# Input norm and first taps on GpSimd, output norms on ScalarE, 4 KB read-back, PSUM banks from a table, a new order

## The chip, the cores and the metric

The kernel runs on one core of a Trainium2 chip. A core has five engines that run at the same time, each with its own instruction queue, taken strictly in order: TensorE (PE; weight loads are shown as PEld), VectorE (DVE), ScalarE (ACT), GpSimd (POOL) and SyncE (SP), which here only issues DMA transfers. Engines wait for one another through semaphores. The metric is the device time of one execution in microseconds; the median of several executions counts.

## The reference

The input `x` is [16, 256, 64, 64] in float32: 16 images, 256 channels, 4096 pixels. Two layers, each added to its input:

```python
# --- layer 0: linear attention ---
x = x + _L0_conv_ref(_gn(x), g_norm, w_qkv, w_out, b_out, g_out)
# --- layer 1: two of four experts for each image ---
x = x + _L1_conv_ref(_gn(x), router_w, router_b, dw_w, dw_b, pw_w, pw_b)
```

`_gn` is a group norm over 32 groups of 8 channels. Layer 0 scales every pixel to unit length over its channels, projects it to q, k and v (4 heads of 32), takes a softmax of q over the head's channels and of k over the pixels, forms a 32 x 32 context for each head, multiplies, projects back to 256 channels and scales every pixel to unit length again. Layer 1 takes the mean over the pixels, a small router, the best two of four experts, and adds their weighted sums; an expert is a 3 x 3 depthwise convolution, GELU (the exact one) and a 256 x 256 pointwise product:

```python
def _expert(x, dw_k, dw_b, pw_k, pw_b):
    h = conv_depthwise_3x3(x, dw_k) + dw_b
    h = gelu(h, approximate=False)
    return einsum('bchw,oc->bohw', h, pw_k) + pw_b
```

## The kernel before

`block_kernel` checks whether the logits of the softmax stay small enough for exponentials without a maximum; they do here, and `pipelined_path` is what runs. `general_path` stands in the program but is not executed.

`pipelined_path` writes its order out by hand. Every step is a small function that issues a few instructions (`norm`, `turn_x`, `out_norm`, `tap1`, ...). A list of rows says which steps exist for which image `b`, group of 512 pixels `g` (8 in an image), quarter of the image `j` (4) or half `h` (2). `place` gives each row a due time from the table `PLAN` (about 3100 entries, many for one image and one group alone), the rows are sorted by it (line 1648), and the instructions are issued in this order. An image has `PERIOD` = 64 units; several images are under way at once: while image b goes through the experts, image b+1 is in the attention and image b+2 is being read for its statistics. So every engine's queue mixes work of up to three images, and the sorted order decides what stands behind what.

The steps that matter here, in the order of one image:

- `load_a` and `load_b` (lines 974, 977): the image is read twice from HBM, in pieces of 128 channels x 512 pixels (`xa` for the statistics, `xb` for the norm), and a third time by `load_x1` into `ring`, a ring of 7 quarter images in which the residual is kept and the output is built.
- `stats` (982) and the steps up to `gn0_bias`: scale `sc` and bias `bi` of the first group norm, one of each for every channel.
- `norm` (1019): `xg = xb * sc + bi`, on VectorE for images 0 and 1 (`EARLY`) and on ScalarE for the other 14; two instructions of 128 x 512 for a group.
- `turn_x` (1030) transposes `xg` on TensorE into the bank `px`; `x_squares` (1039) and `token_scale` (1055) make the pixel's scale `r`, the latter on GpSimd, by a multiply and a power (lines 959 and 960); `x_keep` (1046) writes the scaled transposed pixels to `xt`.
- `project` (1060) makes q and k (bank `pq`), `evacuate` (1071) takes the exponential with scale `r` on ScalarE into `e`, `context` (1079) accumulates on TensorE; `q_sum` (1092, VectorE), `q_norm` (1097, GpSimd), `q_turn` (1103, TensorE, bank `ptq`) and `q_keep` (1109, ScalarE) prepare the normalised q.
- `mix_a` to `mix_c`: once for an image, the context times the output weights (`mw`).
- `attend` (1155): TensorE, two tiles of 128 x 256 into the bank `po`. `out_squares` (1164) on ScalarE and `out_scale` (1172) on GpSimd make the scale `s`. `out_norm` (1176): `ob = po * s`, on ScalarE (two instructions of 128 x 256, line 1181) for images 0, 1 and 15, on VectorE (one of 128 x 512, line 1183) for the other 13; 16 tiles of 128 x 512 in an image.
- `out_turn` (1185) transposes `ob` back (bank `tr`), `out_add` (1193) adds it to `ring` on VectorE, `square_sums` (1202) gathers the second group norm's sums on ScalarE.
- Router: `gn1_sums` to `pick_bias`, short instructions, mostly on VectorE. The chosen experts' weights are fetched by `fetch`, `lace` (GpSimd copies them into `taps`) and `fetch_pw`.
- First 128 channels of the depthwise convolution, on TensorE: `pad0` writes the normalised, padded image; `lay` (1379) stores it in HBM; `spread` (1384) reads it back as overlapping patches into `xr`, in two transfers for each half of the partitions (48 and 6 rows); `conv0` (1422) multiplies by the banded `taps` into the banks `dw`; `gelu0` (1441); `put` (1446) stores the result in the HBM buffer `hids`; `take` (1454) reads it back with the channels on the partitions into `hp`, in four transfers for a half image, each of 32 partitions with one row of 4096 numbers (16 KB) for a partition.
- Second 128 channels, on VectorE: `pad1` (1402); `start1` (1464) writes the first tap with the bias, `acc = pd1 * ds0 + bias`, 128 x 1024, on ScalarE; `tap1` (1472) adds the other eight taps, 128 x 1024 each, two tensors in SBUF as inputs; `gelu1` (1479) on ScalarE.
- `pointwise` (1484): for each quarter and each 128 output channels, the products of both experts and both halves of the channels into two banks `pw`; `residual` (1512) adds bias and residual on VectorE into `ring`; `store` (1520).

All PSUM tiles but the context's come from one pool of 7 banks, `bank` (971), which hands them out in turn: a new tile takes the bank of the tile seven requests earlier and waits until that tile's last reader is done.

Of the kernel before, what the change touches and what calls it, by code (L numbers as in the profile page):

```python
# [10 lines left out]
FP = mybir.dt.float32  # L11
AF = mybir.ActivationFunctionType
ALU = mybir.AluOpType
# [3 lines left out]
P = 128  # L17
# [32 lines left out]
NU = P // (2 * CB)  # L50
NXR = 4
# [9 lines left out]
    "load_x1": 2.02, "mean": 1.19, "means": 13.36, "dev": 13.73, "devs": 17.34, "scale": 17.85,  # L61
    "bias": 21.91, "in_lead": 26.39, "norm0": -8.96, "norm1": -3.87, "turn_x0": 0.72, "x_sq0": 1.77,
    "x_sq1": 2.31, "turn_x1": 1.43, "x_sq2": 3.45, "x_sq3": 3.25, "token": 4.42, "x_keep0": 5.53,
    "x_keep1": 5.77, "x_keep2": 5.97, "x_keep3": 6.03, "project0": 3.18, "evacuate0": 6.05,
    "project1": 3.64, "evacuate1": 6.46, "project2": 3.67, "evacuate2": 6.47, "project3": 4.06,
    "evacuate3": 6.58, "context": 9.48, "q_sum": 8.22, "q_norm": 11.06, "q_turn": 14.73,
    "q_keep": 16.31, "mix_a": 9.53, "mix_turn": 10.09, "mix_v": 11.08, "mix_vv": 11.63,
    "mix_b": 11.82, "mix_out": 13.35, "mix_c": 13.91, "mix_lead": 16.02, "attend0": -1.14,
    "out_sq0": -0.04, "out_sq1": 0.35, "out_scale0": 0.42, "out_norm0": 1.58, "attend1": -0.28,
    "out_sq2": 1.31, "out_sq3": 1.37, "out_scale1": 3.18, "out_norm1": 4.28, "out_turn0": 5.64,  # L70
    "out_add0": 6.51, "sq_sums0": 8.92, "out_turn1": 6.16, "out_add1": 7.06, "sq_sums1": 9.17,
    "sums1": 9.6, "means1": 9.77, "scale1": 10.52, "router": 10.97, "route": 11.89, "choose": 13.68,
    "pick_taps": 21.03, "route_lead": 21.97, "weigh": 29.78, "pick_bias": 41.15, "pad1": -10.35,
    "start0": -0.53, "tap01": 1.33, "tap02": 1.57, "tap03": 1.59, "tap04": 1.87, "tap05": 2.54,
    "tap06": 4.55, "tap07": 4.74, "tap08": 6.14, "gelu10": 13.51, "start1": 1.94, "tap11": 3.52,
    "tap12": 8.13, "tap13": 8.14, "tap14": 8.54, "tap15": 9.95, "tap16": 12.84, "tap17": 13.06,
    "tap18": 14.42, "gelu11": 15.46, "pw00": 16.32, "pw01": 16.45, "pw02": 17.78, "pw03": 17.83,
    "pw10": 16.09, "pw11": 16.24, "pw12": 19.85, "pw13": 20.43, "residual00": 19.8,
    "residual01": 20.37, "store0": 32.19, "residual10": 22.5, "residual11": 23.44, "store1": 26.19,
    "in_first": 0.96, "in_more": 1.71, "q_first": 3.46, "out_first": 27.07, "out_more": 37.75,  # L80
    "q_less": 0.19, "load_a0": -17.62, "load_a1": -6.91, "load_b0": -15.96, "load_b1": -6.67,
    "stats0": -13.55, "stats1": -1.94, "load_weights": 58, "scale_weights": -7.03,
    "end_pw00": 135.48, "end_pw01": -49.35, "end_pw02": 69.96, "end_pw03": 337.87,
    "end_residual00": 3.29, "end_residual01": 66.1, "end_pw10": 115.56, "end_pw11": -47.98,
    "end_pw12": -196, "end_pw13": -114.87, "end_residual10": -13.43, "end_residual11": 88.85,
    "x_0": 0.99, "x_1": -0.21, "x_2": -0.19, "x_e1": 5.09, "x_e2": 4, "route_0": -3.83,
    "route_1": 0.32, "route_2": -0.55, "route_e1": -1.2, "route_e2": -0.21, "out_0": -5.81,
    "out_1": -0.4, "out_2": 0.09, "out_e1": -1.85, "out_e2": -0.87, "q_0": -7.21, "q_1": -2.22,
    "q_2": 0.4, "q_e1": -1.65, "q_e2": -0.57, "in_0": -22.93, "in_1": 7.98, "in_2": 2.65,
    "in_e1": -1.58, "in_e2": 0.28, "pw04": -112.48, "pw14": -23.18, "x_last": 16.71,  # L90
    "v_last": 15.93, "v_e1": 3.4, "tap18@e2.3": 12.73, "start0@e1.3": -0.55, "x_sq2@2.2": 2.88,
    "gelu11@e1.2": 17.06, "tap03@0.1": 1.97, "project0@0.0": 2.01, "out_norm1@2.7": 4.71,
    "out_sq1@e2.0": 0.64, "out_scale1@1.2": 2.19, "evacuate0@1.2": 5.17, "context@1.7": 8.38,
    "out_scale1@0.0": 4.74, "q_norm@0.0": 15.63, "out_turn0@1.4": 5.23, "token@2.1": 4.75,
    "project0@2.7": 3.47, "context@0.7": 8.6, "attend1@e1.3": -2.08, "out_norm1@1.1": 3.87,
    "context@2.1": 7.79, "q_norm@0.6": 12.94, "out_norm0@1.1": 1.4, "gelu11@e2.3": 13.29,
    "evacuate2@1.7": 6.62, "out_norm1@0.6": 4.18, "evacuate2@2.2": 6.81, "project0@2.3": 4.02,
    "token@2.2": 4.19, "norm0@0.0": -14.16, "q_sum@0.0": 10.99, "x_sq2@2.6": 2.62,
    "norm1@0.0": -4.28, "out_norm1@e1.1": 5.78, "x_sq2@1.2": 2.18, "tap04@e2.2": 2.29,
    "x_keep0@0.5": 6.43, "out_turn0@1.2": 5.58, "evacuate3@1.7": 8.13, "x_sq2@2.5": 2.77,  # L100
    "turn_x0@0.0": -3.93, "out_scale0@1.2": 2.15, "tap13@2.0": 6.26, "x_keep3@1.2": 6.99,
    "out_turn0@1.3": 4.82, "q_sum@e2.6": 8.44, "x_sq2@0.0": -1.29, "scale1@0.0": 11.1,
# [2183 lines left out]
```

## Time and profile before

| | |
|---|---|
| time, median of 4 executions | 2672.95 us (2670.32 to 2678.6) |
| the profiled execution's own time | 2679.25 us |
| its span, first to last instruction | 2677.5 us |
| granted TensorE clock, mean | 0.964 |
| DMA traffic | 581.15 MB, mean 217 GB/s |
| ScalarE, input norm (line 1027) | 224 x 815 ns = 182.5 us |
| ScalarE, first taps (line 1467) | 128 x 1242 ns = 158.9 us |
| ScalarE, output norms (line 1181) | 96 x 480 ns = 40.1 us |
| VectorE, output norms (line 1183) | 208 x 679 ns = 141.2 us |
| VectorE, other taps (line 1474) | 1024 x 1299 ns = 1324.9 us |
| GpSimd, q_norm (line 1099) | 128 x 1250 ns = 159.9 us |

The profile names a group of instructions by its line, engine, operation and tiles: `L1474 DVE ... acc<-pd,ds,acc` is the tap of line 1474, which writes `acc` and reads `pd`, `ds` and `acc`. A wait is written "engine tile line <- engine tile line": the first was idle until the second ended. Busy times count the instruction only, not the wait before it; where an instruction has started and is held up, the hold is within its time. TensorE's matmuls overlap one another, so that its busy time is not time at its peak. The time 0 of windows and of the timeline is the first instruction.

### The profile page before, as it was taken

How to read it: one execution, taken by the hardware profiler on the slowest of the kernel's cores; microseconds unless marked ns; L12 is line 12 of the kernel's file. 1: busy time of each engine (PE TensorE's matmuls, PEld its weight loads, DVE VectorE, ACT ScalarE, POOL GpSimd, SP SyncE). 2: the span in 40 equal slices, each digit the busy share in tenths (PEclk: the TensorE clock that was granted, in tenths of full speed). 3: DMA queues.
4: the chain of work that ended last, by engine and by line, in shares of the span. 5: the costliest groups of instructions: out<-in, count | busy, mean ns of one | idle time of the engine just before them, and what ended most of it. 6: DMA issues, size and time to landing. Idle time of an engine off the chain costs nothing.

```text
span 2677.5 us, 50175 instructions
## 1 busy us (share of the span) xinstructions
PE 2414.6 (90%) x17204; PEld 1614.0 (60%) x17204; DVE 2245.3 (84%) x3489; ACT 2073.0 (77%) x4848; POOL 914.0 (34%) x1217
## 2 busy tenths in 40 slices
PE   6897999989899998989899898999989899997877
PEld 5675666656565665656666565666666566564433
DVE  7566789879888888989888898988888888888887
ACT  3588988878788888978788887888888888885632
POOL 4333343333333333324333233333333443433200
PEclk9898999989999999999999999999989999998999
DMA  4838788878778778877877877787877877866885
GB/s 148 103 123 225 226 230 236 235 216 243 212 225 234 224 229 241 237 222 232 226 228 232 239 227 232 223 235 225 255 215 218 237 212 208 229 184 193 223 223 176
DMA packets 410840, 581.15 MB, mean 217 GB/s; under 512 B 66000, under 2 KB 279504, under 8 KB 406480
## 3 DMA queue, kind: packets, MB, share of 16 engines
q1 hardware_dynamic: 377248, 575.36, 74.9%
q10 hardware_dynamic: 33328, 2.49, 1.6%
q8 instruction: 139, 2.28, 0.4%
q14 instruction: 125, 1.02, 0.1%
HBM read 402.49 MB, written 175.24 MB: 216 GB/s over the span
## 4 chain that ended last, share of the span: by engine, by line
PE 43%; DVE 21%; DMA 16%; ACT 8%; issue 6%; SPq 3%; POOL 3%; DVEq 0%; ACTq 0%; POOLq 0%
PE pw L1503 20%; DVE acc L1474 10%; PE pq L1066 6%; DMA hid<-hx 6%; PE pc L1084 4%; PE dw L1432 4%; PE po L1160 4%; DMA xr<-lay 3%; DMA hp<-hid 3%; PE tr L1188 2%; PE px L1035 2%; DVE ob L1183 2%; DVE ring L1518 2%; DMA out<-ring 2%; DVE ring L1197 2%
## 5 line engine op out<-in xcount | busy, mean ns | idle before, releaser
L1474 DVE SCALAR_TENSOR_TENSOR acc<-pd,ds,acc 128x1024 f32<-128x1024 f32 x1024 | 1324.9, 1299 | 44.4 <-ACT acc L1467 28.9
L1503 PE MATMUL pw<-acc,ps 128*128 128x512 f32 x1024 | 496.4, 623 | 25.9 <-ACT acc L1482 23.5
L1503 PE MATMUL pw<-hp,ps 128*128 128x512 f32 x1024 | 479.1, 603 | 22.7 <-DMA hp<-hid 14.8
L1066 PE MATMUL pq<-wqkv_n,xg 128*128 128x256 f32 x2048 | 486.9, 384 | 12.8 <-ACT e L1074 3.5
L959 POOL TENSOR_SCALAR s<-ss 128x2 f32<-128x2 f32 x256 | 128.3, 501 | 1030.5 <-ACT junk L1168 1025.2
L1066 PEld LDWEIGHTS pq<-wqkv_n,xg 128*128 128x128 f32 x2048 | 382.4, 191 | 89.5 <-issue 19.2
L1503 PEld LDWEIGHTS pw<-acc,ps 128*128 128x128 f32 x1024 | 191.8, 199 | 226.7 <-issue 153.8
L1503 PEld LDWEIGHTS pw<-hp,ps 128*128 128x128 f32 x1024 | 188.7, 192 | 208.9 <-issue 197.5
L1042 ACT ACTIVATE jx<-px 128x256 f32<-128x256 f32 x512 | 196.4, 384 | 130.9 <-PE px L1035 121.5
L1160 PE MATMUL po<-mw,qt 128*128 128x256 f32 x1024 | 268.3, 392 | 8.8 <-DVE ring L1197 2.8
L1518 DVE SCALAR_TENSOR_TENSOR ring<-pw,bs,ring 128x512 f32<-128x512 f32 x248 | 180.8, 743 | 113.5 <-PE pw L1503 110.1
L1084 PE MATMUL pc<-xt,e 128*128 128x257 f32 x1024 | 254.4, 391 | 2.5 <-ACT xt L1053 1.7
L1197 DVE SCALAR_TENSOR_TENSOR ring<-tr,gout,ring 128x512 f32<-128x512 f32 x256 | 187.0, 745 | 82.7 <-PE tr L1188 77.8
L1074 ACT ACTIVATE e<-pq,r 128x256 f32<-128x256 f32 x512 | 210.7, 477 | 57.4 <-PE pq L1066 43.6
L1168 ACT ACTIVATE junk<-po 128x256 f32<-128x256 f32 x512 | 197.8, 386 | 70.7 <-PE po L1160 61.8
L960 POOL TENSOR_TENSOR s<-s,mhalf 128x2 f32<-128x2 f32 x256 | 243.7, 952 | 21.4
L1432 PE MATMUL dw<-xr,taps 55*32 55x128 f32 x8192 | 189.3, 287 | 62.3 <-DMA xr<-lay 29.6
L1188 PE MATMUL tr<-ident,ob 128*128 128x128 f32 x1024 | 164.8, 289 | 67.0 <-DVE ob L1183 45.7
L1160 PEld LDWEIGHTS po<-mw,qt 128*128 128x128 f32 x1024 | 187.9, 195 | 61.4 <-issue 22.2
L1432 PEld LDWEIGHTS dw<-xr,taps 55*32 55x32 f32 x8192 | 130.9, 110 | 149.0 <-issue 29.3
L1444 ACT ACTIVATE hx<-dw 128x512 f32<-128x512 f32 x256 | 148.8, 595 | 87.9 <-PE dw L1432 58.4
L1084 PEld LDWEIGHTS pc<-xt,e 128*128 128x128 f32 x1024 | 192.6, 196 | 33.9 <-issue 5.2
(146 smaller groups left out, 3537.1 us busy)
## 6 DMA issues: line engine op xcount, KB each, us to landing
xr<-lay SPq DMA_DIRECT2D x512, 197.6 KB
hid<-hx SPq DMA_DIRECT2D x256, 256.0 KB
hp<-hid SPq DMA_DIRECT2D x128, 512.0 KB
out<-ring SPq DMA_DIRECT2D x128, 512.0 KB
xa<-in_x SPq DMA_DIRECT2D x240, 256.0 KB
xb<-in_x SPq DMA_DIRECT2D x240, 256.0 KB
ring<-in_x SPq DMA_DIRECT2D x120, 512.0 KB
lay<-pd SPq DMA_DIRECT2D x32, 1188.0 KB
```

The lines of the kernel that those rows point to most:

```text
L960: nc.gpsimd.tensor_tensor(out_t, out_t, mhalf[:, :n], ALU.pow)
L1066: nc.tensor.matmul(pq, xg[:, k, c * P : (c + 1) * P], wqkv[:, k, : 2 * HID], start=(k == 0), stop=(k == KH - 1),)
L1074: nc.scalar.activation(live["e", b, g][:, c], live["pq", b, g, c // 2][:, c % 2], AF.Exp, scale=live["r", b, g][:, c : c + 1],)
L1084: nc.tensor.matmul(live["pc", b], live["e", b, g][:, c, HID:], xt[g % 2][:, c], start=(g == 0 and c == 0), stop=(g == NG - 1 and c == CG - 1),
L1160: nc.tensor.matmul(po[:, c], qt[:, n * P : (n + 1) * P], live["mw", b], start=True, stop=True)
L1168: nc.scalar.activation(junk[:, :C], live["po", b, g, hf][:, c], AF.Square, accum_out=ss[:, c : c + 1])
L1188: nc.tensor.transpose(tr[:, c * P : (c + 1) * P], live["ob", b, g, c // 2][:, c % 2, k * P : (k + 1) * P], ident,)
L1197: nc.vector.scalar_tensor_tensor(xin, live.pop(("tr", b, g, k)), gout[:, k : k + 1], xin, ALU.mult, ALU.add, accum_out=live["sm", b][:, 0, ...
L1432: nc.tensor.matmul(pair[r][g * 2 * QR : (g + 1) * 2 * QR, s * HC : (s + 1) * HC], taps[ks, CB * t + i].rearrange("p i x -> p (i x)"), stri ...
L1474: nc.vector.scalar_tensor_tensor(acc, pd1[j % 2][:, t // 3 : t // 3 + QR, t % 3 : t % 3 + W], live["ds", b][:, i, t : t + 1], acc, ALU.mul ...
L1503: nc.tensor.matmul(po, w, rhs, start=begin, stop=end)
L1518: nc.vector.scalar_tensor_tensor(xo, po, bs, xo, ALU.add, ALU.add)
```

## The change

It has six parts. `norm` goes from ScalarE to GpSimd for images 2 to 15. `start1` goes from ScalarE to GpSimd for all images. `out_norm` runs on ScalarE for all images. `take` reads each partition's 16 KB as four pieces of 4 KB: `hp` is laid out as 4 slots of 1024 numbers and 4 unused ones, which keeps neighbouring pieces apart, and `pointwise` (and `band_table`, which borrows the same buffer) address it accordingly. `bank` takes the number of its bank from a table of 1776 digits, one for each request, and no longer in turn. `PLAN` has new due times throughout (3101 entries, 2856 of which stand under the same keys as before). The change's short name also speaks of patches in two transfers; `spread` is the same in both versions.

```diff
+HR = QR // 2 * HC
...
 PLAN = {
-    "load_x1": 2.02, "mean": 1.19, "means": 13.36, "dev": 13.73, "devs": 17.34, "scale": 17.85,
...
+BANKS = (
+    "012345601235601423410563214062305413456012314063521403606321531504262413604215502364105126"
...
+)
...
     def band_table():
 
-        tb = work.tile([P, TOPK * QR * HC], FP, tag="hp", name="bands", bufs=1)
-        tb = tb[:, : NE * KP * QR]
+        tb = work.tile([P, 2 * TOPK, HR + 4], FP, tag="hp", name="bands", bufs=1)
+        tb = tb.rearrange("p s n -> p (s n)")[:, : NE * KP * QR]
...
     live = {}
+    turns = iter(BANKS)
...
     def bank(*key):
-        return banks.tile([P, 512], FP, tag="bank", name="_".join(map(str, key)))
+        tag = f"bank{next(turns)}"
+        return banks.tile([P, 512], FP, tag=tag, name="_".join(map(str, key)), bufs=1)
...
         if b < EARLY:
             nc.vector.tensor_scalar(live["xg", b, g][:, k], xb, sc, bi, ALU.mult, ALU.add)
         else:
-            nc.scalar.activation(live["xg", b, g][:, k], xb, AF.Identity, bias=bi, scale=sc)
+            nc.gpsimd.tensor_scalar(live["xg", b, g][:, k], xb, sc, bi, ALU.mult, ALU.add)
...
     def out_norm(b, g, hf):
         ob = new(work, [P, 2, C], "ob", b, g, hf, bufs=3)
         s, po = live.pop(("s", b, g, hf)), live.pop(("po", b, g, hf))
-        if b in (0, 1, NB - 1):
-            for c in range(2):
-                nc.scalar.activation(ob[:, c], po[:, c], AF.Copy, scale=s[:, c : c + 1])
-        else:
-            nc.vector.tensor_tensor(ob, po, s.unsqueeze(2).to_broadcast([P, 2, C]), ALU.mult)
+        for c in range(2):
+            nc.scalar.activation(ob[:, c], po[:, c], AF.Copy, scale=s[:, c : c + 1])
...
         if ("hp", b, h) not in live:
-            new(work, [P, TOPK * QR, HC], "hp", b, h, bufs=1)
+            new(work, [P, 2 * TOPK, HR + 4], "hp", b, h, bufs=1)
         c0 = r * P // 2 + P // 4 * v
         cs = slice(c0, c0 + P // 4)
         nc.sync.dma_start(
-            out=live["hp", b, h][cs].rearrange("c k x -> c (k x)"), in_=hids[h][cs]
+            out=live["hp", b, h][cs, :, :HR], in_=hids[h][cs].rearrange("c (s n) -> c s n", n=HR)
         )
 
     def start1(b, j, i):
         ds = live["ds", b]
         acc = new(work, [P, QR, W], "acc", b, j, i, bufs=NACC)
-        nc.scalar.activation(
-            acc, pd1[j % 2][:, 0:QR, 0:W], AF.Identity,
-            bias=ds[:, i, 9:10], scale=ds[:, i, 0:1],
+        nc.gpsimd.tensor_scalar(
+            acc, pd1[j % 2][:, 0:QR, 0:W], ds[:, i, 0:1], ds[:, i, 9:10], ALU.mult, ALU.add
         )
...
                 i = part - TOPK
                 w, hp = live["ps", b][:, 0, i, ms], live["hp", b, j // NB2]
-                rhs = hp[:, i * QR + rows.start : i * QR + rows.stop, j % NB2 * W : (j % NB2 + 1) * W]
+                rhs = hp[:, 2 * i + q, :HR].rearrange("p (r x) -> p r x", x=HC)
+                rhs = rhs[:, :, j % NB2 * W : (j % NB2 + 1) * W]
             nc.tensor.matmul(po, w, rhs, start=begin, stop=end)
```

## The prediction

> **What bounds the kernel now.** I read the page's busy times first, then the busy times cut into head, steady part and tail, then TensorE's waits in those stretches, then the sources of the engines that the change touches.
>
> ```profile
> PE 2414.6 (90%) x17204; PEld 1614.0 (60%) x17204; DVE 2245.3 (84%) x3489; ACT 2073.0 (77%) x4848; POOL 914.0 (34%) x1217
> 300.00:2380.00 2080.00, 1936.89 (x14059) 1303.26 (x14059) 1808.16 (x2776) 1729.51 (x3985) 740.85 (x953) 0.97 0.79 228
> 0.00:300.00 300.00, 242.60 (x1385) 190.29 (x1386) 192.41 (x397) 203.92 (x596) 118.80 (x191) 0.95 0.64 155
> 2380.00:2677.00 297.00, 235.10 (x1762) 120.45 (x1760) 244.72 (x318) 139.59 (x271) 54.31 (x73) 0.92 0.74 207
> ```
>
> The first line is the page's part 1. The others are stretches of the span: length, then PE, PEld, DVE, ACT, POOL busy, granted clock, DMA share, GB/s. TensorE is the fullest, and the diff takes no matmul away. What can be won is its idle time: 2080 - 1936.9 = 143 us in the steady part (13 images), 57 in the head, 62 in the tail. VectorE follows with 1808/2080 = 87%, ScalarE has 83%, GpSimd 36%. Who makes TensorE idle in the steady part is the next view (us in total, times, longest):
>
> ```profile
> PE tr L1188 <- DVE ob L1183: 45.7, 30, 4.1
> PE dw L1432 <- DVE ob L1183: 16.3, 7, 2.5
> PE dw L1432 <- DMA xr<-lay: 14.2, 14, 2.7
> PE pw L1503 <- DMA hp<-hid: 6.2, 5, 1.8
> ...
> PE ptq L1107 <- ACT e L1074: 5.6, 9, 1.0
> PE pw L1503 <- ACT acc L1482: 5.0, 5, 2.8
> ```
>
> The output norm on VectorE (`out_norm`, L1183) is the one large entry. `tr` needs its result; `dw` does not read `ob`, so that wait is for the PSUM bank which the norm has to empty.
>
> **Output norms to ScalarE.** 208 VectorE instructions go (141.2 us in part 5, 679 ns each), 416 ScalarE ones come, at 480 ns from the same norm's row in images 0, 1 and 15: +199.7 us. The norm itself gets slower (2 x 0.48 = 0.96 us against 0.68); the hope is in the queue, because on VectorE it stands behind taps of 1.3 us. TensorE's waits on L1183 are 45.7 + 16.3 + 2.4 + 0.8 + 0.5 = 66 us, 0.32 a tile. On L1181 they are 11.5 us over 48 tiles, 0.24 a tile, all of it in head and tail:
>
> ```profile
> L1181 ACT ACTIVATE ob<-po,s x96: 452/473/574, 110.1 to 2526.7; 128x256 f32<-128x256 f32 x96
> ...
>   PE tr L1188: 11.5, 10
> ```
>
> So the gain lies between (0.32 - 0.24) x 208 = 16 us and all 66. ScalarE will be emptier than VectorE was (below), so I take the middle, -40.
>
> **Input norm and first tap from ScalarE to GpSimd.** ScalarE loses 224 x 815 ns = 182.5 us (L1027) and 128 x 1242 ns = 158.9 us (L1467); with the +199.7 it ends 142 us lower, near 1931 (72%). TensorE's steady waits on ScalarE's other work (`e` 7.7, `acc` 5.0, `hx` 4.8, `qt` 0.9) are 18 us, so this relief is worth 0 to 18; I take -5. GpSimd has no row of this instruction. It reads one tensor, like the copy: 239 ns for 64 columns and 1037 for 1024, undisturbed, which is 0.83 ns a column: 0.61 and 1.04 us for 512 and 1024 columns. Upper end, the two-tensor multiply L1099: 1.05 us for 512, so about 2.1 for 1024. I take 0.65 and 1.08, by the copy: 224 x 0.65 + 128 x 1.08 = 284 us, at most 504.
>
> **What that does to VectorE.** The two engines get in each other's way. Here one `q_norm` on GpSimd (1.05 us undisturbed) takes 1.81, and two taps beside it 3.26 instead of 2.56:
>
> ```profile
> 1165.01 3.26 DVE L1474 SCALAR_TENSOR_TENSOR acc<-pd,ds,acc 128x1024 f32<-128x1024 f32 x2
> ...
> 1165.38 1.81 POOL L1099 TENSOR_TENSOR e<-e,qs 128x512 f32<-128x512 f32 x1
> ```
>
> In the records of the taps, the 564 with no GpSimd work beside them take 1278 ns on average, the 31 with only a `q_norm` 1703. All taps together lose 22.6 us over 1290 ns each, almost all to 160 GpSimd instructions of 1.04 us (128 `q_norm`, 32 copies of `taps`): 0.14 us for each. By size that is 128 x 0.14 + 224 x 0.09 = 38 us of the 141 that VectorE was given. If every new instruction stopped a tap for its whole length it would be up to 504 us, and VectorE would bound the kernel. I take 38 by the nearest row; VectorE ends near 2142 (80%). Its cover is that 20%. Only the tail has none, where VectorE is the chain: 8 first taps, each waiting half a running tap (0.64) and stopping the next (0.4), against 1.24 hidden on ScalarE: +4 us, bounds 0 to +9.
>
> The Trainium skill, "SBUF — State Buffer", section "Who interferes with whom", speaks against this part: a VectorE instruction with two SBUF inputs, as the taps are, and a GpSimd instruction that reads SBUF hold a shared port exclusively, and the later one waits for the whole of the other. The trace agrees on who collides (1703 against 1278 ns), but the loss per instruction is a seventh of its length. An estimate by that page, with taps running 1324.9/2677.5 = 49% of the time: 0.49 x 284 = 139 us, and VectorE would have gained nothing.
>
> **What waits on GpSimd's queue.** It is in order. Behind a norm or a first tap now stand the token scales `r` (x_keep and evacuate on ScalarE wait for them), the output scales `s` (the norms) and `q_norm` (TensorE's `ptq`). The waits for `r` and `s` today: xt 21.7 + ob 33.6 + ob on ScalarE 15.3 + xt on VectorE 13.9 + e 6.0 = 90.5 us. GpSimd goes from 914 to 914 + 284 + 352 x 0.49 x 0.64 (half a tap, where one runs) = 1308, 49%. GpSimd is busy with a new instruction 394/2677 = 15% of the time; a scale that meets one waits 0.6 us on average: 384 x 0.15 x 0.6 = 35 us, on an engine with over 20% idle. For TensorE I take +6, bounds 0 and 60 (each of 384 scales late by 0.16).
>
> **Read-back in pieces of 4 KB.** 512 KB to 32 partitions, today in 32 runs of 16 KB. In the packet records a 16 KB run takes 1120 ns, one of 4096 bytes 193, one of 4216 bytes 242: per DMA engine 2 x 1120 = 2.24 us become 8 x 193 to 242 = 1.5 to 1.9 us. TensorE waits 14.8 us for `hp` in all. Issue costs the same on SyncE (its instruction takes 360 ns here; `put`, with 512 runs, 384). Bounds -15 and +5; I take -4. "Patches in two transfers" is in both kernels: `spread` (L1384) is not in the diff, and its 512 + 512 transfers stay.
>
> **Banks by table, new order.** Today a tile takes the banks in turn and may wait for the seventh before it. Waits of TensorE whose releaser is only the last reader of a bank (`dw`, `pq`, `po`, `px`, `tr` on ring L1197 and L1518 and on hx) are about 20 us besides the 16.3 counted above. A table can save them or add as many: -20 to +20, I take -5. The new due times move everything by up to a few us; in the head and tail (57 and 62 us idle; largest `pw` <- gelu 18.5) I find no reason for either sign: 0, bounds -15 and +15.
>
> **Sum.** -40 - 5 + 4 + 6 - 4 - 5 = -44 us on the profiled 2679.25 (span 2677.5): 2635. The median of the runs, 2672.95, lies 6.3 below that execution, so 2629; I say 2630.
>
> **Rivals.** (1) *Slower: late scales.* GpSimd holds `s` and `r` back, the 66 us of waiting stays and is only called ACT ob instead of DVE ob (0 in place of -40), and the late scales cost TensorE 35 to 60 (in place of +6): -44 + 40 + 29 to 54 = +25 to +50, so 2698 to 2723, and less if in part: 2680 to 2725. For it: 0.96 us of norm against 0.68, GpSimd's two-step scale already 0.23 + 0.71 us and stretched by taps, and 33.6 us of VectorE waiting for it. Against: ScalarE has room, and GpSimd sat 1025 us waiting for ScalarE's squares. It decides once TensorE's added waiting passes 44 us, 0.11 us a scale. (2) *Nothing:* the norm is as late on ScalarE as L1181's 0.24 a tile (-16), banks and read-back bring nothing: -16 - 5 + 4 + 6 = -11, about 2662; with half of that given back in the queue, 2668. (3) *More:* all 66, the 18 and half of the banks: -66 - 18 - 10 + 10 = -84, 2589.
>
> **How the numbers follow.** Forecast 0.48 (own range 2605 to 2655), more 0.13, nothing 0.10, slower 0.29. This kernel's measurement tells about 0.2% (5 us) from no change, so 2667.6 to 2678.3 is "same": 0.06 of rival 2, the rest of it counts as faster: 0.65 faster, 0.06 same, 0.29 slower. Range 2588 to 2700: below lies half of (3), above about four tenths of (1), 0.18 together.
>
> **What would show it.** Right: TensorE's waits on `ob` together under 35 us; VectorE near 2140, ScalarE near 1930, GpSimd near 1300; the norm near 0.65 us and the first tap near 1.1 on GpSimd; steady idle of TensorE near 100 us. Wrong: ACT ob <- POOL s grown past 60 us, TensorE waiting for `xg`, taps above 1.36 us on average (that is 60 us lost to the lock), or first taps of 2 us.

## The result, and the profile after

The changed kernel takes 2674.57 us (median of 44 executions, 2657.03 to 2682.7), the kernel before 2675.69 us (70 executions, 2665.99 to 2685.41). The ratio is 0.999 with the interval [0.9982, 0.9998]: 1 us by the medians, 3 us by the ratio, no difference worth the name. 2630 us was forecast; the -44 us did not come. The profiled execution took 2672.99 us, its span is 2671.3 us.

The busy times of the page, part 1, changed kernel:

```profile
PE 2400.1 (90%) x17204; PEld 1597.1 (60%) x17204; DVE 2214.8 (83%) x3281; ACT 1915.8 (72%) x4912; POOL 1430.5 (54%) x1569
```

Its stretches (length, then PE, PEld, DVE, ACT, POOL busy, granted clock, DMA share, GB/s):

```profile
0.00:300.00 300.00, 242.15 (x1396) 191.40 (x1397) 197.97 (x399) 192.65 (x589) 142.18 (x215) 0.95 0.66 157
300.00:2380.00 2080.00, 1927.64 (x14127) 1290.42 (x14126) 1769.28 (x2572) 1606.81 (x4077) 1201.18 (x1268) 0.98 0.82 228
2380.00:2671.00 291.00, 230.31 (x1685) 115.26 (x1683) 247.55 (x311) 116.30 (x247) 87.16 (x87) 0.90 0.74 206
```

TensorE is idle for 58, 152 and 61 us in the three stretches; it was 57, 143 and 62. The stretch in which the gain was expected has given no idle time back: TensorE's idle time there went from 143 to 152 us, and the same 2080 us hold 14127 matmuls in place of 14059. VectorE lost only 30 us of work (2245.3 to 2214.8) though 141 us were taken from it, and GpSimd gained 516 us.

Who makes TensorE wait, steady part, changed kernel (us, times, longest):

```profile
PE pw L1523 <- DMA hp<-hid: 46.6, 22, 3.4
PE pw L1523 <- DVE ring L1217: 21.8, 10, 3.5
PE tr L1208 <- ACT ob L1203: 13.8, 11, 2.5
PE pw L1523 <- ACT xt L1076: 7.4, 6, 1.7
PE px L1058 <- DVE ring L1538: 6.7, 8, 1.5
PE dw L1452 <- DMA xr<-lay: 5.7, 8, 2.3
```

The entry that the change aimed at did shrink. The waits of `tr` and `dw` on `ob` were 45.7 + 16.3 us here before; now `tr` has 13.8. Over the whole span all waits on `ob` are 30.8 + 3.6 + 2.5 + 0.9 + 0.7 + 0.6 = 39 us, where they were 66 on VectorE's norm and 12 on ScalarE's, 78 together. Two other entries took the place: the read-back `hp` (6.2 to 46.6) and `pw` waiting for a bank that `out_add` (L1217) must first empty (1.1 to 21.8).

The groups that moved or were hit, part 5 of the same page (busy us, mean ns of one, then idle before them):

```profile
L1493 DVE SCALAR_TENSOR_TENSOR acc<-pd,ds,acc 128x1024 f32<-128x1024 f32 x1024 | 1418.7, 1391 | 49.1 <-POOL acc L1487 32.2
...
L1487 POOL TENSOR_SCALAR acc<-pd,ds 128x1024 f32<-128x1024 f32 x128 | 211.3, 1650 | 232.0 <-PE pw L1523 224.1
L1050 POOL TENSOR_SCALAR xg<-xb,sc,bi 128x512 f32<-128x512 f32 x224 | 289.1, 1291 | 57.8 <-DMA xb<-in_x 22.7
...
L1203 ACT ACTIVATE ob<-po,s 128x256 f32<-128x256 f32 x512 | 215.0, 477 | 79.8 <-POOL s L981 78.0
```

The 1024 taps take 1391 ns each where they took 1299: +94 us. The new GpSimd instructions are 2.0 and 1.5 times as long as estimated (1291 ns for 650, 1650 for 1080). And ScalarE waits for the scales that now stand behind them; its waits, whole span:

```profile
ACT ob L1203 <- POOL s L981: 78.0, 67, 7.8
ACT xt L1076 <- POOL r L981: 75.0, 57, 4.8
```

With `xt` and `e` (24.0 and 7.8 us on VectorE and ScalarE) all waits for `r` and `s` are 185 us, against 90.5.

The chain that ended last, by engine:

```profile
PE 37%; DVE 21%; DMA 19%; ACT 11%; POOL 6%; issue 4%; SPq 1%; ACTq 0%; DVEq 0%; POOLq 0%
```

Before, TensorE had 43% of it, transfers 16%, ScalarE 8% and GpSimd 3%. The chain is about as long as before; links of it have gone from TensorE to transfers, ScalarE and GpSimd.

### The profile page after: what moved, and what is told of

The parts are those of the page before. It is cut to its first block, busy times and chain, and to the rows that moved or that the text cites. A ratio compares the mean times of both kernels' runs of the same rounds, so it can differ in the third digit from the quotient of the medians.

```text
span 2671.3 us, 50244 instructions
## 1 busy us (share of the span) xinstructions
PE 2400.1 (90%) x17204; PEld 1597.1 (60%) x17204; DVE 2214.8 (83%) x3281; ACT 1915.8 (72%) x4912; POOL 1430.5 (54%) x1569
## 3 DMA queue, kind: packets, MB, share of 16 engines
q1 hardware_dynamic: 389536, 575.36, 76.8%
q14 instruction: 124, 1.02, 0.1%
## 4 chain that ended last, share of the span: by engine, by line
PE 37%; DVE 21%; DMA 19%; ACT 11%; POOL 6%; issue 4%; SPq 1%; ACTq 0%; DVEq 0%; POOLq 0%
PE pw L1523 18%; DVE acc L1493 12%; DMA hp<-hid 7%; DMA hid<-hx 7%; PE pq L1089 5%; PE pc L1107 4%; PE dw L1452 3%; PE po L1183 3%; PE px L1058 2%; DVE ring L1217 2%; DVE st L1007 2%; ACT jx L1065 1%; DVE ring L1538 1%; PE tr L1208 1%; ACT junk L1191 1%
## 5 line engine op out<-in xcount | busy, mean ns | idle before, releaser
L1493 DVE SCALAR_TENSOR_TENSOR acc<-pd,ds,acc 128x1024 f32<-128x1024 f32 x1024 | 1418.7, 1391 | 49.1 <-POOL acc L1487 32.2
L1523 PE MATMUL pw<-hp,ps 128*128 128x512 f32 x1024 | 494.0, 620 | 67.1 <-DMA hp<-hid 54.0
L1523 PE MATMUL pw<-acc,ps 128*128 128x512 f32 x1024 | 491.8, 626 | 47.9 <-DVE ring L1217 21.8
L1089 PE MATMUL pq<-wqkv_n,xg 128*128 128x256 f32 x2048 | 494.7, 385 | 12.8 <-ACT e L1097 7.2
L1089 PEld LDWEIGHTS pq<-wqkv_n,xg 128*128 128x128 f32 x2048 | 376.7, 192 | 81.3 <-issue 15.5
L980 POOL TENSOR_SCALAR s<-ss 128x2 f32<-128x2 f32 x256 | 142.1, 555 | 389.8 <-ACT junk L1191 378.9
L1487 POOL TENSOR_SCALAR acc<-pd,ds 128x1024 f32<-128x1024 f32 x128 | 211.3, 1650 | 232.0 <-PE pw L1523 224.1
L1050 POOL TENSOR_SCALAR xg<-xb,sc,bi 128x512 f32<-128x512 f32 x224 | 289.1, 1291 | 57.8 <-DMA xb<-in_x 22.7
L1203 ACT ACTIVATE ob<-po,s 128x256 f32<-128x256 f32 x512 | 215.0, 477 | 79.8 <-POOL s L981 78.0
L1107 PE MATMUL pc<-xt,e 128*128 128x257 f32 x1024 | 246.2, 382 | 3.9 <-ACT xt L1076 1.7
L1217 DVE SCALAR_TENSOR_TENSOR ring<-tr,gout,ring 128x512 f32<-128x512 f32 x256 | 184.7, 741 | 68.7 <-PE tr L1208 68.4
L1076 ACT ACTIVATE xt<-px,r 128x256 f32<-128x256 f32 x448 | 180.5, 478 | 75.9 <-POOL r L981 75.0
```

What stands on the lines that cost most here:

```text
L1050: nc.gpsimd.tensor_scalar(live["xg", b, g][:, k], xb, sc, bi, ALU.mult, ALU.add)
L1089: nc.tensor.matmul(pq, xg[:, k, c * P : (c + 1) * P], wqkv[:, k, : 2 * HID], start=(k == 0), stop=(k == KH - 1),)
L1107: nc.tensor.matmul(live["pc", b], live["e", b, g][:, c, HID:], xt[g % 2][:, c], start=(g == 0 and c == 0), stop=(g == NG - 1 and c == CG - 1),
L1203: nc.scalar.activation(ob[:, c], po[:, c], AF.Copy, scale=s[:, c : c + 1])
L1217: nc.vector.scalar_tensor_tensor(xin, live.pop(("tr", b, g, k)), gout[:, k : k + 1], xin, ALU.mult, ALU.add, accum_out=live["sm", b][:, 0, ...
L1487: nc.gpsimd.tensor_scalar(acc, pd1[j % 2][:, 0:QR, 0:W], ds[:, i, 0:1], ds[:, i, 9:10], ALU.mult, ALU.add)
```

## The experiments

All ratios are to the kernel before, with 95% intervals; 0.004 is 11 us. "Table" is the list of banks, "order" the new due times. Where only images 3 to 12 are changed, the change for all images was not tried.

**1. The 4 KB read-back.** The changed kernel, with the read-back again in 16 KB rows (the layout of `hp` and what reads it go back with it):

```diff
...
-            out=live["hp", b, h][cs, :, :HR], in_=hids[h][cs].rearrange("c (s n) -> c s n", n=HR)
+            out=live["hp", b, h][cs].rearrange("c k x -> c (k x)"), in_=hids[h][cs]
...
```

> The changed kernel with the read-back again in 32 runs of 16 KB for a transfer; all else as changed. Theory A (the 4 KB pieces are slower and make TensorE wait for hp, 54 us in the changed kernel against 15 before): the waits fall back towards 15 us and the time falls by 20 to 40 us, to about 2640. Rival B (the new order lets the read-back come too late, whatever its pieces): the waits stay near 54 us, the time stays within 5 us of 2674. Rival C (4 KB pieces do help): the waits grow past 60 us, the time rises by 5 to 20 us.

2665.77 us, 0.9948 [0.9928, 0.9967]. The interval lies wholly below that of the changed kernel (0.999 [0.9982, 0.9998]): the pieces cost 0.4%, 11 us. But `hp` still holds TensorE up for 44.7 us (54.0 before that), so most of these waits come from somewhere else. Another thing that differs is the issue (ns min/median/max), changed kernel:

```profile
L1480 SPq DMA_DIRECT2D hp<-hid x128: 537/578/1718, 252.8 to 2635.8; - x128
```

and with 16 KB:

```profile
L1480 SPq DMA_DIRECT2D hp<-hid x128: 302/388/1606, 252.6 to 2635.7; - x128
```

128 x 190 ns = 24 us more on SyncE; whether it lies in the 11 us no run shows. The 4 KB read-back put alone into the kernel before:

> The kernel before with the read-back in pieces of 4 KB, all else as before. Theory A (the pieces take longer on the DMA engines, 302 ns each against 1120 for 16 KB in the two records, as the 11 us between the changed kernel and the one with 16 KB runs say): TensorE's waits for hp grow from 15 us by 3 to 15, the time rises by 3 to 15 us. Rival B (that was the new order's late read-back alone): within 3 us of before.

2678.72 us, 0.9996 [0.9981, 1.001], `hp` waits 15.3 us (14.8 before), although the issue there takes 570 ns too. In the old order the pieces cost nothing that can be told from zero. That this is because the read-back is not late there would fit, but is not shown.

**2. Other parts undone in the changed kernel.** Banks in turn again:

```diff
-        tag = f"bank{next(turns)}"
-        return banks.tile([P, 512], FP, tag=tag, name="_".join(map(str, key)), bufs=1)
+        return banks.tile([P, 512], FP, tag="bank", name="_".join(map(str, key)))
```

> The changed kernel with the PSUM banks handed out in turn again, all else as changed. Theory A (the table makes pw wait for banks held by tr: 22 us of waits on the residual add of layer 0 that were not there before): those waits go, the time falls by 5 to 20 us. Rival B (the table fits the new order and saves waits): waits of TensorE on the last readers of banks grow by 20 us or more, and the time rises by 10 to 60 us.

2702.53 us, 1.0073 [1.0046, 1.01]. Steady waits of TensorE in it:

```profile
PE pw L1522 <- ACT xt L1075: 29.9, 28, 3.7
PE pw L1522 <- DMA hp<-hid: 24.3, 18, 3.9
```

In turn, `pw` gets banks whose last reader is `x_keep` (29.9 us; 7.4 with the table). In this order the table is worth 0.0083 x 2676 = 22 us.

Output norms of images 3 to 12 again on VectorE:

```diff
-        for c in range(2):
-            nc.scalar.activation(ob[:, c], po[:, c], AF.Copy, scale=s[:, c : c + 1])
+        if not 3 <= b <= 12:
+            for c in range(2):
+                nc.scalar.activation(ob[:, c], po[:, c], AF.Copy, scale=s[:, c : c + 1])
+        else:
+            nc.vector.tensor_tensor(ob, po, s.unsqueeze(2).to_broadcast([P, 2, C]), ALU.mult)
```

> The changed kernel with the output norms of images 3 to 12 on VectorE again (160 tiles), all else as changed. Theory A (the move was worth what the waits say, 66 us before against 38 after for the whole run): TensorE's waits on the norm grow by 20 us, VectorE gets 108 us more to do, the time rises by 15 to 40 us. Rival B (the norm's place makes no difference, another stage sets the pace): within 5 us of 2674.

2690.75 us, 1.0047 [1.0029, 1.0066]: the move is worth 0.0057 x 2676 = 15 us in the new order. TensorE's waits on `ob` grow from 39 to 58 us here, so in this pair waits and time go together.

Input norm again on ScalarE:

```diff
-            nc.gpsimd.tensor_scalar(live["xg", b, g][:, k], xb, sc, bi, ALU.mult, ALU.add)
+            nc.scalar.activation(live["xg", b, g][:, k], xb, AF.Identity, bias=bi, scale=sc)
```

> The changed kernel with the input norm of images 2 to 15 on ScalarE again; ScalarE gets 182 us more, to about 2100 us. Theory A (GpSimd's reads hold up the taps: taps rose from 1299 to 1391 ns): the mean tap falls by 20 to 45 ns, ScalarE's waits for r and s (153 us) fall by 30 us or more, and the time falls by 5 to 20 us. Rival B (ScalarE's queue is the tighter one, the loss on VectorE is covered): the time rises by 10 to 40 us although the taps get shorter.

2706.14 us, 1.0097 [1.0074, 1.012]. The page's group of taps in it:

```profile
L1493 DVE SCALAR_TENSOR_TENSOR acc<-pd,ds,acc 128x1024 f32<-128x1024 f32 x1024 | 1380.0, 1353 | 54.7 <-POOL acc L1487 36.4
```

The taps win back 39 us and ScalarE's waits for `r` and `s` fall from 153 to 69.0 + 54.1 = 123 us, and still the kernel is 0.0107 x 2676 = 29 us slower, with ScalarE's busy time up from 1915.8 to 2057.3 us. So in this order the norm's part in the held-up taps and the late scales costs less than its place on ScalarE would. What taps and scales cost in all, the run does not show.

First taps of images 3 to 12 on ScalarE, in the changed kernel, and then with the 16 KB read-back as well:

```diff
-        nc.gpsimd.tensor_scalar(
-            acc, pd1[j % 2][:, 0:QR, 0:W], ds[:, i, 0:1], ds[:, i, 9:10], ALU.mult, ALU.add
-        )
+        if not 3 <= b <= 12:
+            nc.gpsimd.tensor_scalar(
+                acc, pd1[j % 2][:, 0:QR, 0:W], ds[:, i, 0:1], ds[:, i, 9:10], ALU.mult, ALU.add
+            )
+        else:
+            nc.scalar.activation(
+                acc, pd1[j % 2][:, 0:QR, 0:W], AF.Identity,
+                bias=ds[:, i, 9:10], scale=ds[:, i, 0:1],
+            )
```

> The changed kernel with the first taps of images 3 to 12 on ScalarE again (80 instructions, 99 us), all else as changed. Theory A (each part fits the order it was placed for, as with the norms and banks, whose undoing cost 16 to 32 us): the time rises by 5 to 25 us. Rival B (first taps on GpSimd lose more in held-up taps than they free on ScalarE): the mean tap falls by 20 to 40 ns and the time falls by 3 to 15 us.

> The changed kernel with 16 KB runs and the first taps of images 3 to 12 on ScalarE: the two undone parts that did not cost time. Theory A (they add: 0 and -11 us): 2660 to 2670, below both kernels. Rival B (with the read-back faster the first taps' place counts): below 2655 or above 2675.

2675.29 us, 1.0002 [0.9984, 1.002], and 2669.16 us, 0.9957 [0.9942, 0.9973]. Either way the first taps make no difference that can be told (1.0002 against 0.999, 0.9957 against 0.9948), though the taps fell to 1362 ns. The pair shows the 4 KB pieces a second time: 0.0045, 12 us.

**3. The engine moves alone, in the old order.** The kernel before with the output norms of images 3 to 12 on ScalarE too:

```diff
-        if b in (0, 1, NB - 1):
+        if b in (0, 1, NB - 1) or 3 <= b <= 12:
```

> The kernel before with the output norms of images 3 to 12 on ScalarE (160 tiles, 320 instructions of 0.48 us), all else as before. Theory A (the forecast's step: the norm waits behind taps on VectorE, which is worth 40 us): TensorE's waits on the norm fall from 66 to 35 us and the time falls by 15 to 30 us. Rival B (parts and order belong together; in the old order ScalarE is too full): ScalarE's other work comes later, and the time is 5 to 30 us above before.

2691.42 us, 1.0052 [1.0033, 1.0071]. The step that was to bring -40 costs 14 us by itself. TensorE's waits in the steady part:

```profile
PE tr L1188 <- ACT ob L1181: 45.3, 18, 3.5
PE dw L1432 <- DMA xr<-lay: 30.7, 24, 2.1
```

The name has changed, the 45 us have not; the longest waits are nearly as long; the 16.3 us of `dw` on `ob` are gone, but the patches, 14.2 us before, are at 30.7. ScalarE is at 2181.9 us (81%) here.

Input norm and first taps on GpSimd (both, all images of the change):

```diff
-            nc.scalar.activation(live["xg", b, g][:, k], xb, AF.Identity, bias=bi, scale=sc)
+            nc.gpsimd.tensor_scalar(live["xg", b, g][:, k], xb, sc, bi, ALU.mult, ALU.add)
...
-        nc.scalar.activation(
-            acc, pd1[j % 2][:, 0:QR, 0:W], AF.Identity,
-            bias=ds[:, i, 9:10], scale=ds[:, i, 0:1],
+        nc.gpsimd.tensor_scalar(
+            acc, pd1[j % 2][:, 0:QR, 0:W], ds[:, i, 0:1], ds[:, i, 9:10], ALU.mult, ALU.add
         )
```

> The kernel before with the input norm of images 2 to 15 and all first taps on GpSimd, all else as before. Theory A (the forecast: GpSimd's queue costs TensorE 6 us and ScalarE's relief gains 5): within 10 us of before. Rival B (GpSimd holds the scales back and its reads hold up the taps): the mean tap goes from 1299 to about 1390 ns, the waits for r and s from 90 to over 170 us, and the time rises by 20 to 60 us.

2730.28 us, 1.0211 [1.019, 1.0231]: +56 us. ScalarE's longest waits in it:

```profile
ACT junk L1168 <- PE po L1160: 161.5, 95, 10.6
ACT acc L1481 <- DVE acc L1473: 135.7, 42, 16.1
ACT jx L1042 <- PE px L1035: 130.8, 64, 15.4
ACT xt L1053 <- POOL r L960: 128.0, 68, 7.4
```

Before, these four were 61.8, 76.3, 121.5 and 21.7 us. `x_keep` waits 128.0 us for the token scales and TensorE waits for it in turn (`tr` on `xt`, 23.8 us in the steady part); `out_squares` waits 100 us more for `po`, `gelu1` 59 us more for the taps, which are at 1363 ns. All waits for `r` and `s` are 200 us, against 90.5. This looks like the rival of the late scales, but no run separates them from the held-up taps.

Both diffs of this part together:

> The kernel before with all three moves between engines at once (output norms of images 3 to 12 to ScalarE, input norms and first taps to GpSimd), in the old order, with banks in turn and 16 KB runs. Alone the first cost 14 us and the other two 56. Theory A (the moves relieve one another: ScalarE ends 112 us lower, so the output norm no longer comes late): the time is 10 to 35 us above before. Rival B (the costs add up: late scales from GpSimd delay the norms too): 55 to 90 us above before, waits of ScalarE for r and s over 180 us.

2711.58 us, 1.0096 [1.0073, 1.0118]: all three moves without order, table and pieces make the kernel about 26 us slower. Against the GpSimd moves alone (1.0211) the output norms' move now gains 0.0115, 31 us, where by itself it lost 14; ScalarE is at 1895.1 us here, against 2181.9. The waits for `r` and `s` are 182 us, nearly as long as without that move, so shorter waits for the scales hardly explain these 31 us.

The counterpart is the changed kernel with the table and the new order, but the old engines in images 3 to 12 and the 16 KB read-back:

> The new order and the bank table with the old engines in images 3 to 12 (input norm and first taps on ScalarE, output norm on VectorE) and 16 KB runs. Theory A (the order is made for the engines' new shares; each undone move cost up to 32 us): 25 to 60 us above before. Rival B (the new order and the table are better by themselves): at or below before, 2645 to 2676.

2681.11 us, 1.0011 [0.9995, 1.0026]: the same time as before. From here the moves in those ten images lead to 0.9948 (experiment 1), which is -17 us, and the pieces from there to 0.999, +11 us. So order and table with the old engines in most images bring nothing, the moves alone lose, and the moves with order and table gain a little, which the pieces mostly give back.

**4. When the read-back is issued.** `hp` waits grew most, so the read-back was placed 1.5 units (of 64 for an image) earlier, never before its own stores; 16 KB rows:

```diff
+    def due(b, g, key):
+        own = PLAN.get(f"{key}@{nears[b]}.{g}", PLAN[key])
+        if key.startswith("take"):
+            v, r = int(key[4]), key[5]
+            own = max(own - 1.5, due(b, g, f"put{2 * v}{r}"), due(b, g, f"put{2 * v + 1}{r}"))
+        return own
...
-        own = PLAN.get(f"{key}@{nears[b]}.{g}", PLAN[key])
+        own = due(b, g, key)
```

> The changed kernel with the read-back in 16 KB runs and due 1.5 units earlier (3.7 us; never before the stores that it reads). Theory A (the new order's late read-back causes the waits for hp, 45 to 54 us, and they cost time): the waits fall under 25 us, and the time is 10 to 30 us below the changed kernel with 16 KB runs, 2635 to 2655. Rival B (the read-back stands in SyncE's queue and an earlier place only holds up the input loads behind it): SyncE's waits on the store's landing grow from 121 to over 160 us, and the time stays within 6 us of that kernel or rises.

2795.66 us, 1.0459 [1.0432, 1.0485], the largest effect of all. SyncE's own waits in it (us, times, longest):

```profile
SPq L1480 <- DMA hid<-hx: 334.6, 70, 8.3
SPq L998 <- DVE st L1007: 156.0, 56, 11.6
```

and in the kernel of experiment 1, whose order differs in this alone:

```profile
SPq L872 <- DMA out<-ring: 191.9, 35, 9.2
SPq L998 <- DVE st L1007: 144.8, 57, 11.0
SPq L1480 <- DMA hid<-hx: 121.0, 59, 5.4
```

A read-back at the head of SyncE's queue waits until its store has landed, and all transfers behind it wait with it: 334.6 us in place of 121.0, and even `hp` itself is later (waits of 85.5 us against 44.7). The late read-back in the new order is not an oversight that can simply be moved.

**5. What does set the pace?** Six kernels, all made from the kernel of experiment 1 (0.9948 [0.9928, 0.9967]). Five leave out a part of the computation or of a transfer, so that one queue or the DMA engines have less to do; the sixth leaves nothing out. First the compute engines.

```diff
...
-                for t in range(1, 9):
+                for t in range(1, 8):
```

> The changed kernel with 16 KB runs, with the eighth of the nine taps' additions left out: 128 instructions, 1.39 us each, 178 us less on VectorE. Theory A (VectorE with its held-up taps has taken over the pace): the time falls by 90 to 180 us. Rival B (TensorE's own work sets it, VectorE's free fifth covers the rest): it falls by less than 30 us. Rival C (all engines are coupled, none is the pace): 30 to 90 us.

```diff
-                at("v", b, j, f"gelu1{i}", gelu1, b, j, i)
```

> The changed kernel with 16 KB runs, without the GELU of the second 128 channels: 128 instructions of 1.06 us and most of their table loads, some 135 to 175 us less on ScalarE. Theory A (ScalarE's queue sets the pace, since undoing the input norm's move cost 29 us): the time falls by 70 us or more. Rival B (ScalarE at 72% is covered): less than 25 us. Rival C (coupled): 25 to 70 us.

```diff
-        for k in range(KH):
+        for k in range(1):
...
-                start=(k == 0), stop=(k == KH - 1),
+                start=(k == 0), stop=(k == 0),
```

> The changed kernel with 16 KB runs, the projection to q and k with half of its input channels: 1024 matmul instructions of 216 ns, 221 us less on TensorE. Theory A (TensorE, 90% busy, is the pace): the time falls by 110 to 220 us. Rival B (TensorE mostly waits, its busy time is padded by overlap): less than 60 us. Rival C (coupled): 60 to 110 us.

| left out | work taken | time, us | ratio |
|---|---|---|---|
| last of the eight other taps | VectorE 2209.6 to 2033.9 us | 2658.85 | 0.9932 [0.9908, 0.9956] |
| second half's GELU | ScalarE 1912.7 to 1721.1 us | 2674.82 | 0.9974 [0.9946, 1.0003] |
| half of the projection | TensorE 2405.3 to 2265.2 us | 2657.82 | 0.9928 [0.9894, 0.9963] |

140 to 190 us of work gone, and none of the three can be told from the kernel that has it all. The busy times with the projection whole and halved:

```profile
PE 2405.3 (90%) x17204; PEld 1599.4 (60%) x17204; DVE 2209.6 (83%) x3281; ACT 1912.7 (72%) x4912; POOL 1434.1 (54%) x1569
PE 2265.2 (85%) x16180; PEld 1420.2 (53%) x16180; DVE 2192.1 (82%) x3281; ACT 1910.2 (72%) x4912; POOL 1433.2 (54%) x1569
```

The amount of TensorE's work, 90% of the span, does not set the time: with 140 us less it is idle for 394 us (2659.7 - 2265.2) in place of 266. The relief is smaller than the 221 us expected because the projection's own matmuls fell by 210 us (496.9 to 286.5) while others grew (`po` from 389 to 408 ns each), in executions with a granted clock of 0.941 to 0.957 against 0.966 to 0.973; what the missing 81 us would have been worth is not shown.

Then the patches: 512 transfers of six rows left out; the same transfers with 64 numbers a row; and 54 rows in one transfer, with the table of taps and the rows in the order that this takes (nothing left out in this last one).

```diff
-            nc.sync.dma_start(
-                out=tile_t[k0 + 3 * QR : k0 + WK, :n],
-                in_=bass.AP(run.tensor, run.offset + QR * su, [[1, 3], [su, 2], run1]),
-            )
```

> The changed kernel with 16 KB runs, without the 512 small patch transfers of 6 rows: 12.6 MB of 581 less, and 512 issues of some 0.7 us, 370 us less on SyncE's queue. Theory A (SyncE's queue, where each transfer waits in order, sets the pace): the time falls by 60 us or more, TensorE's waits for hp (45 us) by 20. Rival B (it is covered): less than 15 us.

```diff
+            short = [run1[0], 64]
...
-                out=tile_t[k0 + 3 * QR : k0 + WK, :n],
-                in_=bass.AP(run.tensor, run.offset + QR * su, [[1, 3], [su, 2], run1]),
+                out=tile_t[k0 + 3 * QR : k0 + WK, :64],
+                in_=bass.AP(run.tensor, run.offset + QR * su, [[1, 3], [su, 2], short]),
```

> The changed kernel with 16 KB runs; the 512 small patch transfers of 6 rows stay but move 64 numbers a row instead of 1054, so 12 MB less at the same number of issues, the output incomplete. Theory A (SyncE's issue time sets the pace): within 8 us of the changed kernel with 16 KB runs, about 2660 to 2668. Rival B (the bytes and landings set it): about 30 us below it, as without the transfers, 2630 to 2640.

```diff
-                    k = 3 * QR + 2 * dx + u - QR
+                    k = 3 * u + dx
...
-                out=tile_t[k0 : k0 + 3 * QR, :n],
-                in_=bass.AP(run.tensor, run.offset, [[su, QR], [1, 3], run1]),
-            )
-            nc.sync.dma_start(
-                out=tile_t[k0 + 3 * QR : k0 + WK, :n],
-                in_=bass.AP(run.tensor, run.offset + QR * su, [[1, 3], [su, 2], run1]),
+                out=tile_t[k0 : k0 + WK, :n],
+                in_=bass.AP(run.tensor, run.offset, [[su, WR], [1, 3], run1]),
```

> The changed kernel with 16 KB runs, all 54 rows of a patch in one transfer (rows in order of the image, the table of taps laid out to match): the full computation, 512 issues of some 0.7 us less on SyncE, all bytes kept. Theory A (SyncE's issue time sets the pace, and the larger transfer lands as fast): 2632 to 2650, below both kernels. Rival B (54 rows spread worse over the DMA engines than 48 and 6): each transfer lands later, TensorE's waits for xr grow from 18 us to over 50, and the time rises by 10 us or more.

| | time, us | ratio |
|---|---|---|
| no six-row transfers (4 executions) | 2635.03 | 0.9825 [0.9774, 0.9875] |
| six rows, 64 numbers each | 2659.84 | 0.9927 [0.9901, 0.9954] |
| 54 rows in one transfer | 2659.56 | 0.992 [0.9894, 0.9946] |

Taking the transfers away altogether is the only relief with a clear effect: 0.0123 x 2676 = 33 us, by the two intervals 18 to 47. Keeping their issue and dropping their bytes gives 0.2%, keeping the bytes and dropping the issue 0.3%, each within the uncertainty of the difference. Nor does the time follow the DMA engines' busy time: the short rows take 41 us from it (76.2% of 2671.7 us to 75.3% of 2649.7 on the queue of SyncE's transfers) for those 0.2%, the run without the transfers 13 us (76.8% of 2633.4) for its 33. The issue is seen in the patch rows, in the kernel of experiment 1 (first the 48 rows of a patch; the six-row form is on line 1417, median 721 ns) and then with 54 rows:

```profile
L1413 SPq DMA_DIRECT2D xr<-lay x512: 565/581/2376, 207.5 to 2625.1; - x171
```

```profile
L1413 SPq DMA_DIRECT2D xr<-lay x512: 731/764/1949, 208.9 to 2615.8; - x171
...
  PE dw L1448: 24.8, 22
```

One patch costs SyncE 764 ns in place of 581 + 721, which is 512 x 0.54 = 275 us less, but TensorE now waits 24.8 us for patches (17.8 for the six rows before). All issue instructions of SyncE together take 986 us in place of 1277. This version computes everything; with 0.992 it is faster than both kernels, though not to be told from the one of experiment 1.

## Why the prediction was wrong

The range of 2588 to 2700 holds the result only because it is wide; 2605 to 2655, which was to hold if the forecast was right, does not, "nothing" was given 0.10 and "same" 0.06. Along the path that the runs allow, with the moves undone in images 3 to 12, the sum is: order and table +3 us (forecast -5), the moves -17 (forecast -40 - 5 + 6 + 4 = -35 for all images), the 4 KB pieces +11 (forecast -4). Step by step:

- **What bounds the kernel: the step that failed.** "What can be won is its idle time", read off TensorE's list of waits, took each named wait as time that comes back when the wait goes; the largest term of the sum, -40 for the output norms, rests on it. The list shows who came last each time, not what sets the pace. The waits on `ob` fell by 39 us (78 to 39), `hp` and a bank took their place within the same stretch, and TensorE's idle time there did not fall (143 to 152 us). Experiment 5 takes 140 us from TensorE, and 176 and 192 us from VectorE and ScalarE, for nothing measurable.
- **Output norms, -40.** "I take the middle" of 16 and 66. The waits fell about as expected (to 39 us in all; "under 35" was the mark). The price did not follow: alone the move costs 14 us, in the new order it is worth 15, each for 10 of the 13 images. One price for both orders does not exist, and in the old order the price hangs on the GpSimd moves too (14 us lost without them, 31 gained with them), so the steps cannot be priced one by one and added up.
- **ScalarE's relief, -5; 1915.8 us busy against 1931 forecast.** The amount was right. Its worth by itself was not measured: a further 192 us off ScalarE brought nothing (no second GELU, 0.9974), but the norm put back on it (141 us) cost 29 us in the new order, and the output norms' move gained only where ScalarE had been relieved. That fits a relief which counts only together with that move.
- **GpSimd's queue, +6, and the lock, +4.** The undisturbed durations were near: 766 ns at least for the norm (0.65 forecast), 1192 for the first tap (1.08). Their length under taps was not: means of 1291 and 1650 ns; GpSimd came to 1430.5 us against 1308. The taps lost 94 us, not 38, so that VectorE ended at 2214.8 and not 2142; the waits for `r` and `s` doubled. The marks set for "wrong" (taps above 1.36 us, ACT ob <- POOL s past 60 us) were both met. In the old order this step costs 56 us where +6 was taken, near the bound of 60. In the new one undoing it brings nothing back: undoing the norm loses 29 us, undoing the first taps changes nothing. The sizes were wrong, but the two moves as such are not what ate the gain in the changed kernel; what shorter holds would have been worth is not shown.
- **The Trainium skill's rule** ("SBUF — State Buffer", "Who interferes with whom"): the prediction's estimate by it was 139 us lost on VectorE, against 38 by the row; 94 us were measured, about halfway. The prediction set a loss of "a seventh of its length" against the rule. That was an average over 160 instructions, most of which delayed no tap (50 of the 1024 took over 1.34 us), and it did not carry over to 352 more; in the single meeting of a tap and a GpSimd instruction the later one does wait for nearly all that is left of the other (last section).
- **4 KB pieces, -4.** The price of one piece failed: 193 to 242 ns were read off other transfers. Here the 4096-byte packets went from a mean of 193 (35840 of them) to 227 ns (52224), which makes an estimated 302 ns for each of the 16384 new ones if the others stayed as they were: 4 x 302 = 1207 ns against 1120 for a 16 KB row. "Issue costs the same" failed too (578 against 388 ns). Measured: +11 us in the new order, 0 in the old.
- **Bank table, -5.** Its bounds of ±20 were nearly right: 22 us in the new order.
- **New order, 0.** With the old engines in images 3 to 12, the order and its table are together worth nothing (1.0011). But this step was priced by itself, and it is what the other steps hang on: with the table it turns the moves from +26 us (1.0096) into -17, though the two sets of images are not quite the same.
- **Rivals.** "Nothing", 2668, was nearest, and its time lies below the median by only 7 us, but its working (norms as late as ever) is not what happened in the changed kernel, so its nearness is luck. The late scales are real (185 us of waits), but what they cost by themselves no run shows.

What sets the pace stays open. Shown is that slices of 140 to 192 us off each of the three busiest compute engines change nothing measurable, that an earlier place of the read-back in SyncE's queue costs 4.6%, more than any other edit changed, and that 512 patch transfers with issue and bytes are worth 1.2%. That it is the loop through SyncE's queue, in which a transfer waits in order for a landing and holds up those behind it, fits this but is argued, not shown: 291 us less issue bought 0.3%, the bytes alone 0.2%, each within what these runs can tell from zero, and how the 1.2% divides between issue, bytes and the time to landing is not known. Also not tried are the new order with the old engines in all images, and a table of banks made for the old order.

## What to carry to other kernels

A list of waits on the fullest engine names who is late, and not what a shorter wait is worth: before pricing one, take a slice of work from each queue, the one that issues transfers among them, and see which, if any, the time follows. In a kernel whose order is written out by hand, the price of moving an instruction belongs to the order: nearly the same three moves cost 26 us in one and brought 17 in another, so forecast the pair, with wide bounds, and not the sum of the parts. And an edit that rides along with a large change deserves its own run: leaving the read-back as it was is worth 11 us, where the whole change brings 1 to 3.

## What the runs showed of the hardware

- How long a transfer's issue instruction takes on SyncE depends on the form of the transfer (medians): 388 ns for 32 rows of 16 KB, 578 ns for the same bytes in pieces of 4 KB, 581 ns for a patch of 48 rows, 721 ns for one of only six, 764 ns for 54.
- Pieces of 4 KB to 32 partitions were no faster than whole rows: an estimated 4 x 302 ns against 1120 (worked out above).
- A tap on VectorE and a GpSimd instruction that reads SBUF hold each other up, and in all but four of the meetings that can be read singly the later one pays. In the changed kernel's records, 287 taps with no GpSimd work beside them take 1277 ns on average, 52 beside a `q_norm` 1913, 67 beside a first tap 1542. There are 35 meetings of one tap with one long GpSimd instruction (`norm`, first tap, `q_norm` or copy of `taps`) and nothing of the other kind beside either. In 16 the tap began first: it takes at most 8 ns more than alone, the GpSimd instruction up to 1.02 us more. In 15 GpSimd began first, by over 60 ns: its instruction takes at most 6 ns more, the tap up to 0.86 us. In the other four GpSimd began 50 ns or less before the tap and paid all the same, over 1.0 us. One of each kind from the changed kernel's timeline (start, length, in us):

```profile
2079.05 2.60 DVE L1493 SCALAR_TENSOR_TENSOR acc<-pd,ds,acc 128x1024 f32<-128x1024 f32 x2
2080.58 2.15 POOL L1487 TENSOR_SCALAR acc<-pd,ds 128x1024 f32<-128x1024 f32 x1 [2.63 <-PE pw L1523]
...
2389.88 1.20 POOL L1487 TENSOR_SCALAR acc<-pd,ds 128x1024 f32<-128x1024 f32 x1
2390.05 2.09 DVE L1493 SCALAR_TENSOR_TENSOR acc<-pd,ds,acc 128x1024 f32<-128x1024 f32 x1
```

In the first pair two taps run one after the other at their usual length, and the first tap on GpSimd, which begins 0.2 us into the second of them, takes 0.95 us more than its 1.20 alone. In the second pair it takes its usual 1.20, and the tap, which begins 0.17 us after it, 0.82 us more.
